# Gathered sums tied to an even beat in a planner that orders a graph layer's instructions

## The chip, the core and the metric

The kernel runs on one core of a Trainium2 chip, in one launch. Times are device microseconds (us) of that core. The core's engines are called as the profile calls them: PE (TensorE, with PEld for its weight loads), DVE (VectorE), ACT (ScalarE), POOL (GpSimd, which here issues the indirect loads) and SP (SyncE, which issues most plain loads and stores).

## The reference

One graph layer on 6250 nodes of 128 features, with 100000 edges sorted by their target `dst`; each edge has one of two types.

```python
Xs = X[src]
m_data = Xs @ W_data.T + b_data
m_ctrl = Xs @ W_control.T + b_control
msg = jnp.where((edge_types == 0)[:, None], m_data, m_ctrl)
agg = jax.ops.segment_sum(msg, dst, num_segments=X.shape[0])
out = relu(agg + (X @ W_self.T + b_self))
result = layernorm(x + out)        # no scale, no shift, eps 1e-5
```

## The kernel before

**A table first.** Both messages of all 49 blocks of 128 nodes are computed (`multiply`, L465) and split into three bfloat16 parts, so that a message is a row of 384 bfloat16 numbers. The rows stay on the chip as `m3` and are also stored to memory as `table`. This takes the first 80 us or so.

**Then 49 target blocks, in two ways.** An edge's message is added into its target's row by multiplying with a matrix of zeros and ones ("hot"); sums are accumulated in PSUM.

- Blocks 0 to 34, in seven groups of five, here called the p stream. Edges are first put into buckets by their source block (`ranks`, `fill_a`, `fill_b`, `fill_c`, on PE and DVE; few edges that don't fit are fetched by an indirect load, step `spilled`, L715). Then each block has 25 tiles: PE gathers 128 messages with a product out of `m3` (step `g`, tile `g_ps`, L775), ACT copies them from PSUM to `gs` (step `e`, L790; in the last five blocks DVE takes a part), and PE adds them up (step `s`, tile `agg`, L231).
- Blocks 35 to 48, here called the gathered stream: 14 blocks of 18 tiles, 252 in all. POOL fetches 128 rows of `table` by an indirect load (step `msg`, L877) into one of `MB = 5` buffers, DVE makes the hot matrix of six tiles at a time (step `gh`, L889), and PE adds (step `gm`, tile `agg_g`, L231). A tile's sum needs no copy by ACT, so these sums fill PE beside the p stream.

A step `g`, `s` or `gm` is four matmuls of 32 columns with 384 numbers each. After a block's last sum come `whole` and `sum` (DVE), and for each group `root` (DVE), `rooted` (ACT), `scale` (DVE), `apply` (ACT, one per block) and the store `out`. The gathered blocks are normalised in groups of 5, 5 and 4; of the p stream's last group, four blocks go first and block 34 goes alone.

**What sets the order.** Each engine executes its instructions in the order in which the program has them. That order comes from a small planner, the class `Order`, when the program is built. Every stream is a generator of steps; a step names its engines with costs in us, the steps that it needs, and a `lag` after its end. The planner keeps the time at which each engine is free (`self.free`), and always takes, among the steps of the earliest engine that could start within `CLOSE = 0.1` us of the first, the one with the smallest due time (function `due`). The costs, lags and due times exist in the planner alone: on the chip only the order and the real dependences are left.

For the gathered stream the planner before assumes that POOL needs `PACE = 1.68` us for a load, with the rows there 3.0 us after its start; a sum may be placed as soon as its rows are planned to be there, and its due time lies 5 us after its place in an even row. Each load needs the sum five back, whose buffer it takes:

```python
free = [("gm", *gathered[i - MB])] if i >= MB else [*stored, "idx"]
yield step(("msg", j, k), {"G": PACE}, *free, lag=3.0 - PACE)
```

Of the kernel before, what the change touches and what calls it, by code (L numbers as in the profile page):

```python
# [27 lines left out]
KT = 18  # L28
# [24 lines left out]
CH = 6  # L53
# [5 lines left out]
class Order:  # L59
# [10 lines left out]
    CLOSE = 0.1  # L70

    def __init__(self):
        self.free = dict.fromkeys("TVAGS", 0.0)
        self.end = {}

    def run(self, streams, due):
# [24 lines left out]
def step(name, costs, *needs, lag=0.0):  # L101
    return as_tuple(name), costs, [as_tuple(n) for n in needs], lag


def as_tuple(name):
    return name if isinstance(name, tuple) else (name,)
# [107 lines left out]
def sums_over_windows(ctx, tc, x, xt, edges, w, bias, table, packed, total,  # L214
                      add_parts, finish, load_rows, norm):
    nc = tc.nc
    V, A, G, T = nc.vector, nc.scalar, nc.gpsimd, nc.tensor
# [10 lines left out]
    def by_columns(out, lhsT, rhs, **flags):  # L228

        for c in range(0, P, 32):  # L230
            T.matmul(out[c : c + 32], lhsT[:, c : c + 32], rhs, **flags)  # L231
# [151 lines left out]

    LEAD, BUILT = 6.0, 76
    BLOCK = 13.1
    PACE = 1.68
    AHEAD, FIRST = 26.0, 20

    def due(kind, *i):
        if kind in ("p", "g") and i[0] in ("root", "rooted", "scale", "apply", "out"):  # L390
            n = i[1] + 1
            return BUILT + 10 + (BLOCK * sum(p[2] for p in PIECES[:n]) if kind == "p" else PACE * KT * GQ * n)
        if kind in ("counted", "turned", "first"):
            return 5.0
        if kind == "idx":
            return BUILT - 4
        if kind in ("stores", "built"):
            return BUILT - 6
        each = (BUILT - 8 - LEAD) / NB
        if kind == "xt":  # L400
            return LEAD - 6 + each * at_part[i[0]]
        if kind == "er":
            return 5.0
        if kind in ("total", "totalled"):
            return BUILT + BLOCK * (NPB - 1)
        if kind in ("set", "slots"):
            return 14.0
        if kind == "counts":
            return 9.0 if i[0] == GROUPS[0] else 30.0
        if kind == "set2":  # L410
            return 40.0
        kinds = ("y", "yh", "y1", "ym", "y2", "yl")
        if kind in kinds:
            return LEAD + each * i[0] + kinds.index(kind)
        if kind == "table":
            return LEAD + each * (at_part[i[0]] + PARTS[i[0]]) + 14
        if kind in ("win", "xs", "agg", "o", "whole", "sum"):
            b = i[0]
            begun = BUILT + (BLOCK * b if b < NPB else PACE * KT * (b - NPB))
            if kind == "win":  # L420
                return due("fields", blocks[b][0]) - 8 if b < NPB else BUILT - 20
            if b >= NPB:
                return begun + {"whole": PACE * KT + 2, "sum": PACE * KT + 5}.get(kind, 0)
            return begun + {"whole": BLOCK + 0.5, "sum": BLOCK + 3}.get(kind, 0.3 * BLOCK)
        if kind in ("rows", "sel", "d", "g", "e", "s"):
            of = {"rows": 1, "sel": 1, "d": 2}.get(kind, NS)
            lead = {"rows": -9, "sel": -3, "d": -1, "g": 0, "e": 1, "s": 2}[kind]
            return BUILT + BLOCK * (i[0] + (i[1] / of if len(i) > 1 else 0)) + lead
        if kind in ("gh", "gm", "msg"):
            k = i[1] * CH if kind == "gh" else i[1]  # L430
            return BUILT + PACE * (i[0] * KT + k) + {"msg": 0, "gh": 2, "gm": 5}[kind]
        n = GROUPS[i[0]]
        end = BUILT + BLOCK * STARTS[i[0]] - (AHEAD if i[0] else FIRST)
        span = BLOCK * n if i[0] else 34.0
        begun = end - span
        if kind == "fields":
            return begun - 8
        if kind == "hot":
            return begun + span * i[1] * KC / KT - 4
        if kind in ("tri", "rank", "rest"):  # L440
            return begun + span * i[1] / KT + {"tri": 0, "rank": 0.5, "rest": 1}[kind]
        if kind in ("two", "v"):
            c, k = (i[1], 0) if kind == "two" else divmod(i[1], KC)
            return begun + span * (c + 1) * KC / KT + (2 if kind == "two" else 3 + 0.3 * k)
        return end + ("vs", "vd", "to", "over", "pos", "codes", "posed", "list", "listed",
                      "spilled", "full").index({"packed": "vs"}.get(kind, kind))
# [68 lines left out]
    stored = [("table", g, t) for g in range(len(PARTS)) for t in range(2)]  # L515
# [337 lines left out]
    gathered = [(j, k) for j in range(NG) for k in range(KT)]  # L853
    idx = const.tile([P, NG, KT], I32, name="idx")
# [5 lines left out]
    def gathered_fields():  # L860
        yield step("idx", {"V": 1.8}, ("y", NB * 3 // 4), *[("win", b) for b in range(NPB, NB)])
        shape = [P, NG, KT]
        far = work.tile(shape, I32, name="far_g", bufs=1)
        V.tensor_scalar(far, win_g[:, :, :, 2], 0.0, float(NP), op0=ALU.not_equal, op1=ALU.mult)
        V.tensor_add(idx, far, win_g[:, :, :, 0])
        V.tensor_sub(rel_g, win_g[:, :, :, 1], base[:, NPB:, None].to_broadcast(shape))
        low = work.tile(shape, F32, name="low_g", bufs=1)
        V.tensor_single_scalar(low, rel_g, float(P), op=ALU.is_lt)
        V.scalar_tensor_tensor(low, rel_g, 0.0, low, op0=ALU.is_ge, op1=ALU.mult,
                               accum_out=counts[:, NPG : NPG + 1])  # L870

    def gather_rows():
        for i, (j, k) in enumerate(gathered):
            free = [("gm", *gathered[i - MB])] if i >= MB else [*stored, "idx"]
            yield step(("msg", j, k), {"G": PACE}, *free, lag=3.0 - PACE)
            msgs[j, k] = late.tile([P, D3], BF16, name="msg", bufs=MB)
            G.indirect_dma_start(  # L877
                out=msgs[j, k], out_offset=None, in_=table[:, :],
                in_offset=bass.IndirectOffsetOnAxis(ap=idx[:, j, k : k + 1], axis=0),
            )  # L880

    def gathered_hots():
        chunks = [(j, c) for j in range(NG) for c in range(KT // CH)]
        for i, (j, c) in enumerate(chunks):

            free = [("gm", chunks[i - XB][0], chunks[i - XB][1] * CH + CH - 1)] if i >= XB else []
            yield step(("gh", j, c), {"V": 0.55}, ("msg", j, c * CH), ("counts", CH), *free)
            g_hots[j, c] = hot = late.tile([P, P, CH], BF16, name="hot_g", bufs=XB)
            V.tensor_tensor(hot, counted[CH],  # L889
                            rel_g[:, j, None, c * CH : c * CH + CH].to_broadcast([P, P, CH]),  # L890
                            op=ALU.is_equal)

    def gathered_sums():
        for j, k in gathered:
            free = [("agg", NPB + j)] if k == 0 else [("o", NPB + j)] if k == KT - 1 else []
            yield step(("gm", j, k), {"T": 0.165}, ("msg", j, k), ("gh", j, k // CH), *free)
            if k == 0:
                aggs[NPB + j] = ps_a.tile([P, D3], F32, name="agg_g")
            by_columns(aggs[NPB + j], g_hots[j, k // CH][:, :, k % CH], msgs.pop((j, k)),
                       start=k == 0, stop=k == KT - 1, skip_group_check=True)  # L900

    def finish_gathered():
        for j in range(NG):
            b = NPB + j
            yield step(("whole", b), {"V": 0.5}, ("gm", j, KT - 1))
            whole = add_parts(aggs.pop(b), work)
            yield step(("sum", b), {"V": 0.7}, ("whole", b))
            if j % GQ == 0:
                kept.append((late.tile([P, GQ, D], F32, name="h_g"),
                             work.tile([P, Q, 2], F32, name="mv_g")))  # L910
            h, mv = kept[-1]
            finish(h[:, j % GQ, :], whole, xss.pop(b))
            stats(mv[:, j % GQ, :], h[:, j % GQ, :], work)
# [14 lines left out]
    def close_build():  # L928
# [9 lines left out]
        normalise([(lambda g=g: (hs_[g], mvs[g]), STARTS[g] + q0, q0, n) for g, q0, n in PIECES], "p"), add_up(), gather(), evict(), to_hots(), bucket_hots(),  # L938
        multiply(), take(0, "yh", "y"), leave(0, "y1", "yh"),
        take(1, "ym", "y1"), last_part(), constants(), store(), close_build(), add_counts(),  # L940
        finish_gathered(), gathered_sums(), gathered_hots(), gather_rows(), gathered_fields(),
        normalise([(lambda i=i: kept[i], NPB + i * GQ, 0, min(GQ, NG - i * GQ))
                   for i in range(-(-NG // GQ))], "g"),
        load_own("p", list(range(NPB)), XS),
# [128 lines left out]
```

## Time and profile before

| what | value |
|---|---|
| median of 13 runs | 544.62 us (542.65 to 546.29) |
| profiled execution: its own time | 543.5 us |
| profiled execution: span from first to last instruction | 541.8 us |
| mean granted TensorE clock over the span | 0.986 |
| busy share of the span: PE, PEld, DVE, ACT, POOL | 94%, 82%, 80%, 77%, 55% |
| indirect loads `msg` on POOL | 252, mean 1138 ns each on the engine |
| eviction `gs<-g_ps` on ACT | 807, mean 498 ns |

The busy share is an average over stages: the table until about 80 us, then both streams side by side until the last gathered sum at 517 us, then the end of the p stream. "Idle before" is the time for which an engine stood still ahead of an instruction, with what released it. A matmul's end is modelled, and consecutive matmuls overlap.

### The profile page before, as it was taken

The page shows a single profiled execution, that of the slowest core. Times are in us where ns is not written, and L with a number is a line of the kernel's source. Part 1 is how long each engine was busy: PE and PEld are TensorE (multiplying, and loading weights), DVE is VectorE, ACT ScalarE, POOL GpSimd, SP SyncE. Part 2 cuts the span into 40 slices and gives each one's busy share as a digit, 9 for nine tenths or more (in the row PEclk, how much of TensorE's full clock was granted, in tenths as well). Part 3 has the DMA queues.
Part 4 walks back from the last instruction along what each step waited for, and adds up shares of the span by engine and source line. Part 5 has one row for each costly group of instructions (what it writes and reads, how often), then busy time and mean ns, then how long its engine had stood idle before and what let it go on. Part 6 is the DMA issues. An engine that isn't in the chain of part 4 may idle for free.

```text
span 541.8 us, 26355 instructions
## 1 busy us (share of the span) xinstructions
PE 507.0 (94%) x11204; PEld 442.0 (82%) x11204; DVE 432.6 (80%) x967; ACT 416.0 (77%) x1003; POOL 295.9 (55%) x267
## 2 busy tenths in 40 slices
PE   5799977899989999999999999999999999999993
PEld 3546547799887998988989899989898999988882
DVE  5587879578987789978799878999789667668884
ACT  6654346577869788798888888977879879888894
POOL 1000002677687676777567676775757756676500
PEclk9999999899999999999999999999999999999998
DMA  3566875543555435554354543544445454555301
GB/s 98 142 177 200 259 235 187 153 130 79 184 153 166 136 78 178 158 162 141 98 194 137 165 141 80 183 139 158 142 132 162 130 159 135 182 168 156 116 14 38
DMA packets 60932, 79.19 MB, mean 146 GB/s; under 512 B 15760, under 2 KB 51371, under 8 KB 60807
## 3 DMA queue, kind: packets, MB, share of 16 engines
q1 hardware_dynamic: 47253, 49.14, 27.9%
q0 software_dynamic: 12400, 25.08, 17.7%
q10 hardware_dynamic: 1154, 3.21, 1.9%
q8 instruction: 89, 1.46, 1.1%
q14 instruction: 36, 0.29, 0.2%
HBM read 64.35 MB, written 13.05 MB: 143 GB/s over the span
## 4 chain that ended last, share of the span: by engine, by line
PE 76%; DMA 8%; DVE 7%; ACT 3%; issue 3%; POOL 1%; SPq 1%; ACTq 0%; DVEq 0%; POOLq 0%
PE agg L231 25%; PE g_ps L775 24%; PE acc L231 9%; PE agg_g L231 8%; PE small L621 7%; DMA msg<-table,idx 4%; DMA rows<-packed 3%; PE y L465 2%; DVE slot L584 2%; ACT gs L790 1%; DVE hot_st L567 1%; ACT h_p L189 1%; DVE two L605 1%; ACT h_g L189 1%; POOL msg L877 1%
## 5 line engine op out<-in xcount | busy, mean ns | idle before, releaser
L790 ACT CAST gs<-g_ps 128x384 bf16<-128x384 f32 x807 | 333.7, 498 | 74.7 <-PE g_ps L775 54.7
L877 POOL DMA_INDIRECT msg<-table,idx x252 | 286.8, 1138 | 118.1 <-PE g_ps L775 49.6
L775 PE MATMUL g_ps<-m,rows 128*32 128x384 bf16 x3430 | 322.3, 332 | 0.9 <-ACT gs L790 0.7
L231 PE MATMUL agg<-gs,hot_d 128*32 128x384 bf16 x3360 | 301.0, 330 | 3.3 <-ACT gs L790 3.3
L231 PEld LDWEIGHTS <-hot_d 128*32 128x32 bf16 x3500 | 194.6, 137 | 13.5 <-issue 7.2
L775 PEld LDWEIGHTS <-rows 128*32 128x32 bf16 x3430 | 188.5, 136 | 19.1 <-issue 13.3
L231 PE MATMUL agg_g<-msg,hot_g 128*32 128x384 bf16 x1008 | 109.4, 331 | 7.0 <-DMA msg<-table,idx 6.2
L584 DVE TENSOR_REDUCE slot<-acc 128x5 bf16<-128x490 f32 x126 | 83.5, 663 | 28.9 <-PE acc L231 17.3
L760 DVE TENSOR_TENSOR hot_d<-count,to 128x1664 bf16<-128x1664 bf16 x70 | 74.5, 1065 | 6.6 <-PE agg L231 6.6
L621 PE MATMUL small<-hot_st,two 128*32 128x98 bf16 x1260 | 70.2, 291 | 0.0
L231 PE MATMUL acc<-hot_st,tri 128*32 128x490 bf16 x504 | 62.2, 376 | 2.2 <-DVE hot_st L567 2.2
L231 PEld LDWEIGHTS <-hot_g 128*32 128x32 bf16 x1008 | 53.9, 123 | 11.6 <-issue 8.1
L231 PE MATMUL acc<-hot_st,rest 128*32 128x490 bf16 x476 | 56.7, 379 | 5.2 <-DVE slot L584 4.8
L621 PEld LDWEIGHTS <-two 128*32 128x32 bf16 x1260 | 58.8, 118 | 2.0 <-issue 0.3
L715 POOL DMA_INDIRECT mixed<-table,row_i x7 | 6.8, 969 | 92.9 <-PE g_ps L775 82.4
L476 ACT CAST m<-y 128x512 bf16<-128x512 f32 (+1 forms) x50 | 28.1, 577 | 30.8 <-PE y L483 23.0
L567 DVE TENSOR_TENSOR hot_st<-count,st_b 128x2940 bf16<-128x2940 bf16 x21 | 41.8, 1995 | 7.0 <-PE small L621 5.3
L746 DVE TENSOR_SCALAR rows<-rows,pid 128x3136 bf16<-128x3136 bf16 x35 | 37.2, 1062 | 7.6 <-DMA rows<-packed 6.1
L153 DVE TENSOR_REDUCE whole<-agg 128x128 f32<-128x384 f32 x35 | 19.4, 554 | 17.5 <-PE agg L231 12.4
L465 PE MATMUL y<-w_sb,xt 128*128 128x256 f32 x98 | 33.1, 424 | 0.0
L231 PEld LDWEIGHTS <-rest 128*32 128x32 bf16 x476 | 21.9, 99 | 13.6 <-issue 12.7
L231 PEld LDWEIGHTS <-tri 128*32 128x32 bf16 x504 | 22.4, 99 | 3.3 <-issue 3.1
(144 smaller groups left out, 436.7 us busy)
## 6 DMA issues: line engine op xcount, KB each, us to landing
rows<-packed SPq DMA_DIRECT2D x35, 784.0 KB
table<-m SPq DMA_DIRECT2D x10, 768.0 KB
msg<-table,idx POOLq DMA_INDIRECT x252
xt<-in_xt ACTq DMA_DIRECT2D x5, 512.0 KB
xt_p<-in_xt SPq DMA_DIRECT2D x35, 64.0 KB
xs_p<-in_x SPq DMA_DIRECT2D x35, 64.0 KB
out<-h_p SPq DMA_DIRECT2D x6, 320.0 KB
table<-m SPq DMA_DIRECT2D x2, 480.0 KB
```

What stands on the lines that cost most here:

```text
L153: nc.vector.tensor_reduce(whole, agg.rearrange("p (i c) -> p c i", i=3), axis=AX.X, op=ALU.add)
L231: T.matmul(out[c : c + 32], lhsT[:, c : c + 32], rhs, **flags)
L465: T.matmul(y[:, j, :], xts[g][:, b + j - at_part[g], :], w_sb[:, : 2 * D], start=j == 0, stop=False, skip_group_check=True)
L476: A.copy(part_of(b, n, i), ys[b][:, :n, :].rearrange("p b (t c) -> p t b c", t=2))
L567: V.tensor_tensor(hot, counted[n][:, None, 1 : NT + 1, :].to_broadcast([P, KC, NT, n]), fields[grp][2][:, c * KC : c * KC + KC, None, :].t ...
L584: V.tensor_reduce(slots[grp][:, k, :], by_q, axis=AX.X, op=ALU.max)
L621: T.matmul(vt[c0 : c0 + R, q // 2, :], two[:, k % KC, i, :, q], hot[:, k % KC, :, q], start=k == 0 and q < 2, stop=k == KT - 1, skip_group ...
L746: V.tensor_scalar(rows[b], rows[b], pid1, None, op0=ALU.is_equal)
L760: V.tensor_tensor(hot, counted[DC][:, :, :n], places[grp][:, q, None, c * DC : c * DC + n].to_broadcast([P, P, n]), op=ALU.is_equal)
L775: T.matmul(g_ps[t * R : (t + 1) * R, :D3], rows[b][:, :, s], m3[:, s, :], start=True, stop=True)
L790: (A.copy if e == "A" else V.tensor_copy)(gs[at], g_tiles.pop((b, g))[at, :D3])
L877: G.indirect_dma_start(out=msgs[j, k], out_offset=None, in_=table[:, :], in_offset=bass.IndirectOffsetOnAxis(ap=idx[:, j, k : k + 1], axis=0),
```

## The change

The planner gets a sixth, made-up engine "C". A new stream `beats` puts one step every `PACE` us on it, starting 4.0 us after the table's stores are planned to have landed. Each gathered sum needs its beat too, so that it is never planned earlier than that. `PACE` grows from 1.68 to 1.75; the planned cost of a load on POOL falls from 1.68 to 1.25 and its rows are planned to be there 4.25 us after its start; a sum's due time no longer lies 5 us behind its place. The beats issue nothing: the changed kernel has the same instructions on the chip in another order. The wait of each load for the sum five back was there before and is there after.

```diff
-        self.free = dict.fromkeys("TVAGS", 0.0)
+        self.free = dict.fromkeys("TVAGSC", 0.0)
...
-    PACE = 1.68
+    PACE = 1.75
...
+        if kind in ("beat", "beating"):
+            return 0.0
         if kind in ("gh", "gm", "msg"):
             k = i[1] * CH if kind == "gh" else i[1]
-            return BUILT + PACE * (i[0] * KT + k) + {"msg": 0, "gh": 2, "gm": 5}[kind]
+            return BUILT + PACE * (i[0] * KT + k) + {"msg": 0, "gh": 2, "gm": 0}[kind]
...
-            yield step(("msg", j, k), {"G": PACE}, *free, lag=3.0 - PACE)
+            yield step(("msg", j, k), {"G": 1.25}, *free, lag=3.0)
...
+    def beats():
+
+        yield step("beating", {"C": 4.0}, *stored, "idx")
+        for i, (j, k) in enumerate(gathered):
+            yield step(("beat", j, k), {"C": PACE}, "beating")
...
-            yield step(("gm", j, k), {"T": 0.165}, ("msg", j, k), ("gh", j, k // CH), *free)
+            yield step(("gm", j, k), {"T": 0.165}, ("msg", j, k), ("beat", j, k), ("gh", j, k // CH), *free)
...
-        finish_gathered(), gathered_sums(), gathered_hots(), gather_rows(), gathered_fields(),
+        finish_gathered(), gathered_sums(), gathered_hots(), gather_rows(), gathered_fields(), beats(),
```

## The prediction, made before the changed kernel ran

> **What bounds the kernel now.** I read the page's engine rows first, then busy time by stretches, then the list of waits, then PE's timeline around its longest wait, and last the chain of waits at the end. Busy time by stretches (columns: PE, PEld, DVE, ACT, POOL busy with counts, then PE's clock, DMA share, GB/s):
>
> ```profile
> 70.00:140.00 70.00, 62.19 (x1346) 52.94 (x1348) 56.24 (x120) 47.14 (x114) 36.14 (x30) 0.95 0.52 160
> 140.00:210.00 70.00, 67.66 (x1618) 60.79 (x1607) 58.59 (x131) 57.10 (x140) 50.60 (x44) 1.00 0.48 141
> 210.00:280.00 70.00, 68.34 (x1647) 62.58 (x1650) 59.98 (x139) 58.26 (x148) 49.27 (x43) 1.00 0.51 154
> 280.00:350.00 70.00, 69.20 (x1709) 65.00 (x1705) 60.60 (x132) 58.78 (x145) 49.28 (x44) 1.00 0.48 142
> 350.00:420.00 70.00, 68.31 (x1667) 62.72 (x1661) 61.74 (x135) 58.44 (x148) 47.91 (x44) 1.00 0.47 144
> 420.00:490.00 70.00, 69.24 (x1687) 64.22 (x1683) 49.24 (x113) 60.06 (x153) 45.64 (x44) 1.00 0.49 152
> ```
>
> From 140 us on PE stands still for 1 to 3.4% of the time; the next engines are DVE at 70 to 88% and ACT at 82 to 86%. The densest stretch issues 1709 matmuls in 70 us, 0.041 us each, so a step of four takes 0.164 us. Against that rate the stretches 140:210, 210:280, 350:420 and 420:490 lack 91, 62, 42 and 22 matmuls, 217 x 0.041 = 8.9 us (the mix of shapes differs a little, so this is rough). PE bounds the middle; what it waits there is carried to the end. The waits and the timeline of PE (start, duration, in brackets idle before and releaser) say for what:
>
> ```profile
> PE agg_g L231 <- DMA msg<-table,idx: 6.2, 5, 3.6
> PE agg L231 <- ACT gs L790: 3.3, 6, 1.0
> POOL msg L877 <- PE agg_g L231: 38.7, 59, 2.1
> ACT gs L790 <- PE g_ps L775: 54.7, 97, 5.3
> ```
>
> ```profile
> 91.48 0.35 PE L775 MATMUL g_ps<-m,rows 128*32 128x384 bf16 x4
> 95.43 0.38 PE L231 MATMUL agg_g<-msg,hot_g 128*32 128x384 bf16 x4 [3.60 <-DMA msg<-table,idx]
> 96.55 0.45 PE L231 MATMUL agg_g<-msg,hot_g 128*32 128x384 bf16 x4 [0.31 <-DMA msg<-table,idx]
> 105.19 0.38 PE L231 MATMUL agg_g<-msg,hot_g 128*32 128x384 bf16 x4 [0.56 <-DMA msg<-table,idx]
> ```
>
> The largest wait of PE in the two-stream part is for gathered rows: 6.2 us in 5 waits, one of 3.6 us before the very first sum. POOL in turn stands still for sums (38.7 us behind `agg_g`): the load waits for its buffer. And ACT waits for PE 54.7 us, far more than PE for ACT. At the end the chain of waits reads (start, length, what):
>
> ```profile
> 522.94 0.38 ACT h_g L189
> ...
> 523.85 0.49 ACT h_g L189
> ...
> 532.63 0.48 ACT mixed L790
> 533.16 0.41 PE agg L231 x4
> 533.59 0.57 DVE whole L153
> ...
> 535.24 0.21 ACT s L170
> ...
> 536.65 0.49 ACT h_p L189
> ```
>
> After the last gathered sum (517.3 us) evictions on ACT lead, and two of the gathered blocks' `apply` stand among them on the chain. The last eviction starts at 532.63 and ends at 533.10, `whole` of block 34 follows at 533.59, and its store is issued at 537.17, 4.07 us after that eviction.
>
> **The change, part by part.** No instruction is added or removed; costs, lag, beat and due time live in the planner. So the planned 1.25 us for a load costs nothing on POOL and neither does the wait for the sum five back, which the old program has as well. What changes is position, and that can be counted in the built order of PE, in matmuls.
>
> (a) The first gathered sum stands 26 matmuls later (878th instead of 852nd). 26 x 0.041 = 1.05 us of other work moves into the 3.6 us wait, if it is ready: the evictions that it needs run until about 92.5 us (ACT is busy 0.53 us of 92 to 94), while PE had stopped at 91.8. So PE arrives at about 92.8 instead of 91.8; the rows land at 95.4 as before, since the loads ahead of it keep their order. Gain 1.0 us, bounds 0 and 1.05.
>
> (b) The other four waits for rows, 6.2 - 3.6 = 2.6 us. From one gathered sum to the one five later, between which a load has to be issued and land, the old order has 102 matmuls at the least, and under 160 in 21 places of 247; the new order 148 at the least, under 160 in one. At 0.041 us that is 4.2 against 6.1 us. From the trace's semaphore times I read 2.4 to 6.8 us from issue to landing (median 3.6, nine in ten under 5.5), and 0.3 us from a sum's end to the issue. So nearly all gaps now exceed what a load takes. Gain 2.6 us, at least 1.0 (the waits after the first five tiles, 0.31 and 0.56, have 1 to 2.5 us more room), at most 2.6.
>
> (c) The clock. In 96 to 98 and 98 to 100 us the granted clock was 0.68 and 0.50, right after the 3.6 us wait; after the wait of 1.5 us at 159 us it stayed at 1.00. Half speed for 3.4 us costs up to 1.7 us. A wait of 2.6 us lies between those two, so the gain is 0 to 1.7; I take 0, as PE would still be idle from 92.8 to 95.4, most of the same stretch.
>
> The Trainium skill (TensorE: Matmul & The Clock Gate, HAM oscillation) names PE idle gaps over about 3.4 us as what throttles the clock. The row agrees; by the rule alone a wait of 2.6 us would be short enough and the sum below 1.7 us better.
>
> (d) All other waits of PE (3.3 us on evictions, some on `slot`) are dealt anew, since every step moves against every other. Even spacing should rather help: 13 times in the old order two gathered sums stand back to back, once in the new. Upper bound: the 8.9 us lacking in the middle less the 2.0 us of (b) that lie there, so about 7. Lower bound: nothing excludes a loss; the nearest rows are POOL's spilled loads, which hold up the loads behind them by up to 2.9 us, and one such wait hitting PE would cost that. I take 0, with 3 us either way.
>
> [...]
>
> (e) The end of the p stream. In the old order 348 matmuls follow the last gathered sum; they take from 517.3 to 533.5 us, 16.2 us or 0.0466 each, 2.0 us more than at full rate. In the new order 70 follow, so some seven gathered sums (0.164 us each) go into that slack, and the gathered blocks' `apply`, of which the chain has 0.87 us, leave it. Gain 0.9 us, bounds 0 and 2.0.
>
> (f) The last four gathered blocks are now finished at the very end. On DVE their `root` and `scale` stand ahead of `whole` of block 34, and on ACT their `rooted` stands behind the last eviction and their four `apply` ahead of block 34's `rooted`. With e the end of the last eviction, from the old chain's rows: `rooted` until e + 0.26, then 0.27 to the first of six DVE instructions and 1.13 through them, so `whole` at e + 1.7 instead of e + 0.49. Then 1.65 us to `rooted`, e + 3.35; ACT is busy with four `apply` (0.4 apart, the last 0.5 long) until e + 3.45. Then 1.93 us to the store as before, so e + 5.4 instead of e + 4.07. Cost 1.35 us, bounds 0.5 and 2.5. The gathered blocks' own store (245 KB) is issued at about e + 4 and lands some 2 us later (the 256 KB store issued at 531.88 stopped moving data at 533.9), before the last one.
>
> Sum: - 1.0 - 2.6 - 0 - 0 - 0.9 + 1.35 = - 3.15 us. On the profiled execution, 543.5 us (span 541.8 and 1.7 around it), that gives 540.4; this execution lies 1.1 us under the median of 544.62, so in medians 541.5 us. Adding all favourable bounds gives far less than 536, all unfavourable ones 544.62 + 0 - 1.0 + 3 + 2.5 = 549.1; both are unlikely in full.
>
> **Rivals.** *Eviction paces instead (slower).* If the p stream is held by the loop of four `g_ps` buffers and ACT, PE's saved waits come back as waits for `gs`, and (f) stays: 544.62 + 1.35 = 546.0. For it: ACT is at 84 to 86% and leads the end of the chain. Against: ACT waits 54.7 us for PE, PE 4.0 us for ACT. It decides once PE's waits on ACT grow by over 3.6 us, what (a) and (b) bring. Chance 0.22.
>
> *A larger gain.* The clock dip goes (1.7) and a third of the lacking 7 us is filled (2.3): 541.5 - 4.0 = 537.5. For it: 153 of the 217 lacking matmuls are lacking between 140 and 280 us, before the two streams have settled into the dense rate. Against: no wait of PE in the list but those for rows is that large. Chance 0.2.
>
> *It does nothing.* The order moves, but waits for rows reappear behind the spilled loads and take half of (b), and evictions take the rest of what (f) leaves: 544.6. Chance 0.14.
>
> **How the numbers follow.** My own case, 541.5 with 539 to 543.3, has 0.42; the larger gain 0.2, no change 0.14, slower 0.22, with 0.02 for surprises of over 3 us on the slow side. Two executions' medians can be told apart here at about 0.2%, 1.1 us. So faster 0.62, same 0.14, slower 0.24. The range reaches from 536.5 (a little beyond the larger gain) to 546.6 (just beyond the eviction case).
>
> **What would show it.** In the changed profile: PE's waits for `msg` down from 6.2 to about 2.6 us, all in the first; a first gathered sum still near 95.4 us; the last one some 3 to 4 us before PE's end, near 528; `whole` of block 34 1.7 us after the last eviction; the store 5.4 us after it. PE's waits for `gs` should stay near 3 to 4 us: if they reach 7, the eviction rival is right. A clock of 1.00 between 96 and 100 us would speak for the larger gain. If waits for `msg` stay at 6 us, (b) is wrong.

## The result and the profile after

The changed kernel's median is 538.1 us (10 runs, 536.57 to 538.64), against 544.55 us for the kernel before (46 runs, 541.58 to 546.4). The ratio is 0.9878 [0.9861, 0.9895], a gain of 6.45 us. The prediction had 541.5: the sign was right and the value lies inside the range, but the gain is more than twice the 3.15 us of the sum.

The profiled execution of the changed kernel took 538.18 us, its span 536.4 us, 5.4 us less than before. The remaining 1 us of the 6.45 is no change of mechanism: before's profiled execution lay 1.05 us under its own median, the changed one lies at its median. So what has to be explained in the traces is 5.4 us.

First, busy time by stretches of the changed kernel (columns as before: PE, PEld, DVE, ACT, POOL busy with counts, PE's clock, DMA share, GB/s):

```profile
70.00:140.00 70.00, 63.16 (x1380) 54.84 (x1383) 57.62 (x127) 48.92 (x120) 33.34 (x32) 0.95 0.51 163
140.00:210.00 70.00, 68.42 (x1661) 62.96 (x1655) 60.37 (x135) 58.67 (x144) 50.62 (x42) 1.00 0.50 149
210.00:280.00 70.00, 69.14 (x1659) 63.00 (x1655) 59.78 (x133) 58.74 (x147) 50.88 (x44) 1.00 0.50 147
350.00:420.00 70.00, 69.02 (x1713) 63.99 (x1709) 60.25 (x136) 60.32 (x150) 49.81 (x43) 1.00 0.50 149
490.00:520.00 30.00, 30.00 (x734) 28.32 (x730) 24.67 (x49) 23.77 (x56) 17.82 (x16) 1.00 0.38 111
```

PE executes more matmuls in the same time: 1380 instead of 1346 in the first of these stretches, 1661 instead of 1618 in the second, 1713 instead of 1667 in the fourth; 420:490 went the other way, from 1687 to 1653. In 490:520 it is 734, where before had 701:

```profile
490.00:520.00 30.00, 29.38 (x701) 25.63 (x697) 24.90 (x53) 25.35 (x61) 14.76 (x13) 1.00 0.38 117
```

The clock is the same in each of these stretches.

Second, the list of waits (total us, how many, the longest). The lines answer to those of before; the last one is POOL's wait ahead of the spilled loads, which the prediction did not show:

```profile
PE agg_g L231 <- DMA msg<-table,idx: 4.0, 1, 4.0
PE agg L231 <- ACT gs L792: 3.7, 6, 1.0
POOL msg L879 <- PE agg_g L231: 50.5, 75, 2.3
ACT gs L792 <- PE g_ps L777: 55.8, 87, 3.8
POOL mixed L717 <- issue: 1.2, 4, 0.3
```

PE waits for gathered rows once, before the first sum, and not again. Its waits for evictions moved from 3.3 to 3.7 us, so ACT did not become the bound. POOL waits longer for sums than before, 50.5 us against 38.7, at no cost to PE. Before, the spilled loads stood like this in the same view:

```profile
POOL mixed L715 <- DVE dq L712: 8.3, 4, 2.9
POOL mixed L715 <- DVE dq L711: 1.9, 1, 1.9
```

POOL takes its instructions in order. For 10.2 us it stood still at spilled loads whose list of rows DVE had not finished, and every gathered load behind them stood still too. After the change POOL is idle for 0.3 us ahead of each spilled load but the first group's, four of them in the line above.

Third, PE's timeline around its one wait (start, duration, in brackets idle before and releaser):

```profile
92.35 0.40 PE L231 MATMUL agg<-gs,hot_d 128*32 128x384 bf16 x4
96.74 0.38 PE L231 MATMUL agg_g<-msg,hot_g 128*32 128x384 bf16 x4 [3.99 <-DMA msg<-table,idx]
```

Last, the end of the chain of waits (start, length, what):

```profile
527.09 0.48 ACT mixed L792
...
528.05 0.57 DVE whole L153
...
529.70 0.21 ACT s L170
...
531.10 0.49 ACT h_p L189
```

The last eviction ends at 527.56, `whole` of block 34 starts 0.49 us later and its store is issued 4.07 us after that eviction. Before it was 0.49 and 4.07 us too. The four gathered blocks that are now finished here cost the end nothing.

**A finer reading than the list.** A matmul's end is modelled and consecutive matmuls overlap, so the list of waits counts only idle time beyond the modelled end. The trace also has starts. Below, a "start gap" is the time from the start of one matmul to the start of the next, less the 0.165 us of a whole step (0.21 us for the wider ones), where over 0.15 us is left, from 88 us on. How long a gap comes out depends on what is taken off, so the sums compare kernels better than they measure a loss. Before the change the start gaps ahead of gathered sums add up to 8.7 us, 3.76 ahead of the first one and 4.95 ahead of the others; after it 4.15 ahead of the first and nothing ahead of the others. All other start gaps of PE are 14.3 us before and 14.0 after.

### The profile page after: what moved, and what is told of

The parts are those of the page before. It is cut to its first block, busy times and chain, and to the rows that moved or that the text cites. A ratio compares the mean times of both kernels' runs of the same rounds, so it can differ in the third digit from the quotient of the medians.

```text
span 536.4 us, 26363 instructions
## 1 busy us (share of the span) xinstructions
PE 504.8 (94%) x11204; PEld 442.6 (83%) x11204; DVE 431.8 (80%) x968; ACT 416.8 (78%) x1002; POOL 300.8 (56%) x267
## 4 chain that ended last, share of the span: by engine, by line
PE 79%; DVE 9%; DMA 4%; ACT 3%; issue 2%; SPq 2%; ACTq 0%; DVEq 0%
PE agg L231 27%; PE g_ps L777 25%; PE acc L231 9%; PE agg_g L231 8%; PE small L623 7%; PE y L467 2%; DMA rows<-packed 2%; DVE hot_st L569 2%; ACT gs L792 2%; DVE slot L586 2%; ACT h_p L189 1%; DMA msg<-table,idx 1%; DVE two L607 1%; DMA packed<-vs 1%; SPq L809 1%
## 5 line engine op out<-in xcount | busy, mean ns | idle before, releaser
L879 POOL DMA_INDIRECT msg<-table,idx x252 | 290.4, 1153 | 125.4 <-PE g_ps L777 57.4
L777 PE MATMUL g_ps<-m,rows 128*32 128x384 bf16 x3430 | 318.6, 332 | 0.0
L231 PEld LDWEIGHTS <-hot_d 128*32 128x32 bf16 x3500 | 192.5, 137 | 13.6 <-issue 8.9
L231 PE MATMUL agg_g<-msg,hot_g 128*32 128x384 bf16 x1008 | 112.4, 329 | 4.0 <-DMA msg<-table,idx 4.0
L623 PE MATMUL small<-hot_st,two 128*32 128x98 bf16 x1260 | 68.6, 291 | 0.5 <-DVE two L607 0.4
L231 PE MATMUL acc<-hot_st,tri 128*32 128x490 bf16 x504 | 60.6, 374 | 2.3 <-DVE hot_st L569 2.3
L623 PEld LDWEIGHTS <-two 128*32 128x32 bf16 x1260 | 57.0, 118 | 3.4 <-DVE two L607 1.8
L717 POOL DMA_INDIRECT mixed<-table,row_i x7 | 8.1, 1158 | 84.9 <-PE g_ps L777 83.1
L792 DVE CAST gs<-g_ps 128x384 bf16<-128x384 f32 x34 | 18.5, 554 | 8.8 <-PE g_ps L777 5.3
```

The costliest lines, as they stand in the source:

```text
L623: T.matmul(vt[c0 : c0 + R, q // 2, :], two[:, k % KC, i, :, q], hot[:, k % KC, :, q], start=k == 0 and q < 2, stop=k == KT - 1, skip_group ...
L777: T.matmul(g_ps[t * R : (t + 1) * R, :D3], rows[b][:, :, s], m3[:, s, :], start=True, stop=True)
L792: (A.copy if e == "A" else V.tensor_copy)(gs[at], g_tiles.pop((b, g))[at, :D3])
L879: G.indirect_dma_start(out=msgs[j, k], out_offset=None, in_=table[:, :], in_offset=bass.IndirectOffsetOnAxis(ap=idx[:, j, k : k + 1], axis=0),
```

## Experiments

The theory after this reading: the gain is PE's waits for gathered rows, and they vanish for two reasons, because there is more distance between a sum and the one five later (what the prediction had), and because POOL's queue is no longer held up by spilled loads. The rivals: one part of the change does it alone (the pace, or the planned costs without the beat); more buffers would do the same; any new order would have done it; the first wait and the clock decide.

### Which part of the change

**The old pace with all the rest of the change.**

```diff
-    PACE = 1.75
+    PACE = 1.68
```

> The changed kernel with PACE back at 1.68: sums of gathered tiles still on an even beat, but as early as before (412 matmuls follow the last one, 348 in the old kernel, 70 in the changed one). Shortest distance to the sum five later 154 matmuls (old 102, changed 148). Theory, evenness removes PE's waits for gathered rows: most of the gain stays, 4 to 6 us faster than before, waits for rows down to the first one. Rival, the slower pace fills the end of the p stream: at most 1 us faster. Rival, any new order is a draw: anything between -3 and +3 us.

Measured: 539.02 us, 0.9893 [0.9867, 0.9919]. The new pace isn't needed; the interval overlaps that of the whole change, and POOL is idle for 0.3 us ahead of each late spilled load here too.

**The new pace alone, on the kernel before.**

```diff
-    PACE = 1.68
+    PACE = 1.75
```

> The old kernel with PACE 1.75 alone, without beats, old costs and due times: the sums run as late as in the changed kernel (the last one stands at the very end) but unevenly (distance to the sum five later at least 136 matmuls, under 160 in 13 places; old 102 and 21, changed 148 and 1). Theory, evenness: some of the waits for rows stay; 1 to 2 us faster from them, less what the last gathered block now costs at the very end, so -2 to +2 us. Rival, pace and a filled end: 4 to 6 us faster.

Measured: 546.36 us, 1.0038 [1.0018, 1.0058]. By itself the pace costs a little. PE ended at 531.9 us, earlier than before's 533.5, but the last gathered sum stood at the very end of the order, and from PE's end to the end of the span it took 13.4 us instead of 8.3. POOL's wait at the spilled loads was 11.7 us.

**Planned costs, lag and due time, without the beat.** On the changed kernel:

```diff
-    PACE = 1.75
+    PACE = 1.68
...
-            yield step(("gm", j, k), {"T": 0.165}, ("msg", j, k), ("beat", j, k), ("gh", j, k // CH), *free)
+            yield step(("gm", j, k), {"T": 0.165}, ("msg", j, k), ("gh", j, k // CH), *free)
```

> The changed kernel without the beats and with PACE 1.68: planned cost of a load 1.25 and due time not set back, so sums are placed as soon as rows are planned to be there. Distances to the sum five later grow less even (under 150 matmuls in 37 places, 8 in the old kernel). Theory, evenness: waits for rows stay at 6 us or grow; 0 to 5 us slower than before. Rival, the planner's truer costs bring the gain: 4 to 6 us faster.

Measured: 546.07 us, 1.0019 [0.9992, 1.0046]: no gain. PE's waits for rows rose to 11.3 us in 9 waits:

```profile
PE agg_g L231 <- DMA msg<-table,idx: 11.3, 9, 4.3
POOL mixed L717 <- issue: 0.9, 3, 0.3
```

In the built order 53 of the 247 distances to the sum five later are under 160 matmuls, against 21 before and 1 after. Without the beat the planner bunches the sums. POOL, on the other hand, no longer stands at the spilled loads: ahead of each of the six late ones it is idle for 0.3 us. So it is the planned costs, not the beat, that move these out of the way, and that alone does not help.

**The beat, with the old planned cost of a load.** On the changed kernel:

```diff
-            yield step(("msg", j, k), {"G": 1.25}, *free, lag=3.0)
+            yield step(("msg", j, k), {"G": PACE}, *free, lag=3.0 - PACE)
```

> The changed kernel, with beats and PACE 1.75, but POOL planned as before: a load costs PACE and its rows are there 3.0 us after its start. In the built order the sums are less even again (seven back to back, at least 114 matmuls to the sum five later, three places under 160) and 18 matmuls follow the last one. Theory, evenness and the place of the spilled loads in POOL's queue both count: POOL waits for the spilled loads' indices return (8 to 12 us, none in the changed kernel), some waits of PE for rows return; 1 to 4 us slower than the changed kernel. Rival, the beat alone does it: within 1 us of the changed kernel.

Measured: 548.23 us, 1.0071 [1.0046, 1.0096]. The spacing is nearly as even as after (3 distances under 160), but the kernel is slower than before. Part of it is the tail, 11.4 us from PE's end to the end of the span instead of 8.3. More shows in the list of waits:

```profile
PE agg_g L231 <- DMA msg<-table,idx: 10.1, 9, 4.4
POOL mixed L717 <- DVE dq L714: 13.7, 5, 3.4
```

POOL stands 13.7 us behind spilled loads. They execute at 274.72, 341.30, 408.75 and 474.47 us after waits of 2.4 to 3.4 us, and 5 to 6 us after each of them, at 280.8, 346.3, 413.7 and 480.3, PE has a start gap ahead of a gathered sum whose rows come last. So even spacing alone does not do it; these four gaps are the second cause caught in the act.

### Spilled loads and buffers

**Eight buffers, all orders as before.**

```diff
-    MB, XB = 5, 2
+    MB, XB = 8, 2
```

> The old kernel with MB = 8 buffers for gathered rows in place of 5. Every engine's order of instructions is that of the old kernel, only loads may go earlier. Theory, the gain is the waits for rows: PE's waits for rows fall to the first one, and the time falls by what they really cost, 2.6 us by the list of waits, up to 5 us by the gaps between matmul starts. Rival, the gain is the new order itself (evictions, tail): at most 1 us faster.

Measured: 542.44 us, 0.9965 [0.9945, 0.9985], 1.9 us less than before. The built order is that of before on every engine; a load now waits for the sum eight back. If the distance of five were all, the waits for rows would have gone. They stayed at 6.5 us in 6, and POOL, which now can run ahead, ran into the spilled loads:

```profile
POOL mixed L715 <- DVE dq L712: 37.7, 6, 7.5
```

The lead that POOL gains is used up there, and PE's gaps at 213 and 480 us, ahead of gathered sums behind a spilled load, are 0.7 and 0.55 us; before had 0.4 us (in two) and 0.4 us there. All start gaps ahead of gathered sums fell from 8.7 to 7.8 us, about half of the gain; where the other half comes from the trace does not show.

**Eight buffers in the changed kernel** (the same edit).

> The changed kernel with eight buffers for gathered rows in place of five, planned with eight too (two places with under 160 matmuls to the sum five later, 70 matmuls become 86 after the last gathered sum). Theory, in the new order no wait for rows but the first is left, so more room brings nothing: within 1.5 us of the changed kernel, 4.5 to 8 us faster than before. Rival, loads that go earlier always help: 1.9 us faster than the changed kernel, as eight buffers were in the old order.

Measured: 538.35 us, 0.9886 [0.9868, 0.9905]. Once the waits are gone, more buffers bring nothing that can be measured.

**Spilled loads four gathered loads later, all else as before.** Only POOL's order differs from before:

```diff
+    HOLD, held = 4, []
...
-            G.indirect_dma_start(
-                out=mixed[grp % 2][:R], out_offset=None, in_=table[:, :],
-                in_offset=bass.IndirectOffsetOnAxis(ap=row_i[:, 0:1], axis=0),
-            )
+            if grp:
+                held.append([HOLD, mixed[grp % 2][:R], row_i])
+            else:
+                spill(mixed[grp % 2][:R], row_i)
...
+            for one in list(held):
+                one[0] -= 1
+                if not one[0]:
+                    held.remove(one)
+                    spill(*one[1:])
```

> The old kernel, with each spilled load (but the first group's) put four gathered loads later in POOL's queue. Every other engine's order is the old one. Theory, the spilled load at the head of POOL's queue, waiting for its indices from DVE (8.3 and 1.9 us in the old trace), holds up the loads behind it and so makes rows late: POOL's wait for dq falls under 1 us, PE's gaps before gathered sums fall from 8.7 to about 5 us, 2 to 4 us faster than before. Rival, rows are late because sums stand too close together: within 1 us of before.

Measured: 541.79 us, 0.9947 [0.9926, 0.9969], 2.8 us less than before. POOL's wait for `dq` is gone; PE's waits for rows fell from 6.2 to 5.1 us in the list, its start gaps ahead of gathered sums from 8.7 to 6.7, and PE ended 1.5 us earlier, at 532.0. The profiled execution, 542.36 us, gained less than the median; its clock was at half for 6.8 us behind the first wait, before's for 3.4. This is the second cause by itself.

**Spilled loads seven gathered loads later, with eight buffers.** `HOLD` is 7 and `MB` is 8, all else as before.

> As the last one, with eight buffers for gathered rows and the spilled loads seven loads later; all other orders are the old ones. Here rows can hardly be late after the first tiles, whatever the spacing of the sums. Theory, late rows are what the change took away: 3 to 5 us faster than before, PE's gaps before gathered sums near 4.5 us, all at the first tiles. Rival, the new order gains by its even mix of both streams: at most 2 us faster, as eight buffers alone.

Measured: 540.47 us, 0.9923 [0.9894, 0.9952], 4.1 us less than before.

```profile
PE agg_g L231 <- DMA msg<-table,idx: 4.9, 3, 3.5
```

The waits for rows that are left are those of the first three late tiles (3.67 at 94.2, 0.48 at 95.5, 1.08 at 104.3 us); after 105 us no rows were waited for. So with before's order of PE untouched, distance and a free POOL queue bring about two thirds of the gain. (That both together bring more than the later loads alone, 541.79 us, shows in the traces; the two intervals overlap.) About 1 us of what is left to the changed kernel is those first tiles, 5.2 us against 4.2; the other us or so is inside the intervals.

**The beat with the old load cost, and spilled loads four later.** The kernel of 548.23 us, with `HOLD = 4`:

> The kernel with beats and the old planned cost of a load (548.2 us, PE's gaps before gathered sums 12.9 us), with each spilled load four gathered loads later in POOL's queue. Theory, held-up loads cost it: 3 to 6 us faster than without this, so 542 to 545 us; the rest of its loss is its end, where the gathered blocks' normalisation stands behind the last sums. Rival, its uneven sums cost it: within 1.5 us of 548.2.

Measured: 544.57 us, 1.0011 [0.9989, 1.0033], 3.7 us less than without the delay by the medians, 3.3 us by the two ratios. PE's waits for rows fell from 10.1 to 4.7 us, none of the four gaps named above is there, and PE ended at 528.2 us, as early as in the changed kernel (528.0). (The comparison with 538.0 in the kernel without the delay would say too much: of the two profiled executions that one, 551.46 us, was among its slowest, this one, 541.55, its fastest.) What it still loses in its trace is the tail: the last gathered sum stands at the very end of its order (18 matmuls follow it in the same plan), and from PE's end to the end of the span it takes 11.4 us. The 3 us from there to its median no trace shows.

### The first wait, the clock, the pace

**First beat later.** On the changed kernel the beats start 10.0 instead of 4.0 us after the stores, with `PACE` 1.72 in the first of these kernels and 1.68 in the second; the third and fourth start at 8.0 with 1.68 and at 6.0 with 1.75. The edit of the second:

```diff
-    PACE = 1.75
+    PACE = 1.68
...
-        yield step("beating", {"C": 4.0}, *stored, "idx")
+        yield step("beating", {"C": 10.0}, *stored, "idx")
```

> The changed kernel with the first beat 10 us instead of 4 us after the stores and PACE 1.72: the first gathered sum stands 96 matmuls later (974th), distances to the sum five later are as even (one place under 160), 170 matmuls follow the last one. Theory, the first wait of 4 us is PE time lost: it falls to under 1 us and the half-speed stretch behind it with its 1.7 us may go; 2 to 5 us faster than the changed kernel. Rival, before the first sum ACT's evictions pace the p stream anyway, so PE waits for ACT in place of rows: within 1.5 us of the changed kernel.

Measured: 539.75 us, 0.991 [0.9892, 0.9927].

> Beats with PACE 1.68, the first beat 10 us after the stores instead of 4: the first gathered sum is the 974th matmul instead of the 878th, 388 matmuls follow the last one (412 with the first beat at 4 us, 539.0 us). Theory, the first wait of 4 us and the half-speed stretch behind it are lost PE time: first wait under 1 us, clock 1.00 between 92 and 104 us, 1.5 to 4 us faster than with the first beat at 4 us, so 535 to 537.5 us. Rival, ACT's evictions pace the p stream there: PE's gaps before g_ps and agg grow by what the first wait loses, 538 to 540 us.

Measured: 537.93 us, 0.9875 [0.9845, 0.9906].

> As the last one, with the first beat at 8 us: the first gathered sum is the 934th matmul. Theory, lost PE time: the first wait about halved, no half-speed stretch if it is under 2 us; between 536 and 538.5 us. Rival, evictions pace: 538 to 540 us.

Measured: 539.83 us, 0.9901 [0.9869, 0.9932].

> The changed kernel with the first beat at 6 us instead of 4: first gathered sum the 914th matmul, no place under 160 matmuls to the sum five later, 54 matmuls after the last one. Theory, lost PE time: the first wait about 1.5 us shorter, 0.5 to 2 us faster than the changed kernel's 538.1. Rival, evictions pace, or the later end gives it back: 538 to 540 us.

Measured: 537.59 us, 0.9867 [0.9825, 0.9909].

None of the four can be told apart from the changed kernel, though the first wait is down to 1.7 us or less in all of them and the clock stays at 1.00. Two windows around it, first of the kernel with the old pace (first beat at 4.0), then of the one with 10.0 and the same pace:

```profile
96.00:100.00 4.00, 4.00 (x64) 2.62 (x57) 0.77 (x2) 1.40 (x4) 2.90 (x4) 0.63 0.40 108
```

```profile
96.00:100.00 4.00, 4.00 (x108) 3.88 (x107) 3.89 (x6) 2.33 (x7) 2.73 (x4) 1.00 0.55 133
```

From 92 to 100 us PE started 64 matmuls in the one and 163 in the other, so some 99 x 0.041 = 4.1 us of work was done earlier. At 94 us block 0 was done, 5.2 us before the other's 99.2; block 32 was done at 510.1 and 510.8. The lead was lost on the way: PE's start gaps ahead of `g_ps` are 9.9 us instead of 6.5 and those ahead of `acc` grew to 3.3, and all start gaps together are 19 us in both. So in these two traces the first wait, 4 us long, was worth 0.6 us at PE's end (529.1 and 528.5 us) and in the medians about 1 us, with intervals that leave room for 2 us more or less. That the p stream is paced by its four `g_ps` buffers and ACT in the early part would explain it, but no run isolates that. The fourth kernel's trace looks better: it has 15.8 us of start gaps in all, and PE ended at 522.8 us, 5.2 us before the changed kernel's. But this execution, 534.79 us, was one of its fastest (its runs go from 533.97 to 541.15), and its median gains nothing that can be told from none. So what the first wait costs stays open.

**The pace 1.72, first beat as in the change.**

```diff
-    PACE = 1.75
+    PACE = 1.72
```

> The changed kernel with PACE 1.72: 244 matmuls follow the last gathered sum (70 at 1.75, 412 at 1.68), seven places under 160 matmuls to the sum five later. Theory, with beats and true load costs the pace matters little: 537.5 to 539.5 us, as at 1.68 (539.0) and 1.75 (538.1). Rival, each order is a draw of its own: over 541 us or under 536.5 us.

Measured: 542.73 us (539.03 to 546.78), 0.9971 [0.9941, 1.0]. This misses what the theory expected. Its profiled execution, at 546.3 us near the top of its spread, has PE's waits for rows at 5.6 us in 4 and 24.8 us of start gaps in all, against 18.2 in the changed kernel and 19 to 21 in those with a later first beat and the paces 1.68 and 1.72. The pace itself is not bad, since 1.72 with a later first beat gave 539.75. All other kernels here that have both the beat and the new load cost lie between 537.6 and 539.8; this one falls out by 3 to 5 us, and the cause is open. It sets a limit to the theory: an order that does all that the change asks for can still lose most of the gain.

### The end

**The square root behind the evictions.** In the code `root` issues two instructions: an addition on DVE and the square root on ACT. The planner's step `rooted` comes after it and issues nothing. On the changed kernel, the square root is moved into that step:

```diff
-            v, s0 = root(mv, n, work)
+            v = root(mv, n, work, at_once=False)
             yield step((last, "rooted", grp), {"A": 0.3}, (last, "root", grp))
+            s0 = work.tile([P, Q], F32, name="s0")
+            A.activation(s0[:, :n], v[:, :n], AF.Sqrt)
```

> The changed kernel with the square root emitted with the step rooted instead of with root, which is where the prediction took it to be; on ACT it then stands one to three evictions later in every normalised group, and behind the last eviction in the gathered blocks' last group; no other engine's work is added or removed. Theory, this is why part (f) of the prediction cost nothing: whole of block 34 starts about 1.7 us after the last eviction's end instead of 0.5, the store is issued about 5.4 us after it instead of 4.07, and the time is 1.0 to 1.6 us longer than the changed kernel's. Rival, the end was covered by something else: no change.

Measured: 539.23 us (534.65 to 540.82), 0.9885 [0.9849, 0.9922], so in medians it can't be told from the changed kernel. The trace tells them apart. ACT's timeline of the changed kernel:

```profile
526.42 0.27 ACT L170 ACTIVATE s<-v 128x4 f32<-128x4 f32 x1
526.53 0.53 ACT L792 CAST gs<-g_ps 128x384 bf16<-128x384 f32 x1
527.09 0.47 ACT L792 CAST mixed<-g_ps 64x384 bf16<-64x384 f32 x1
527.95 1.65 ACT L189 ACTIVATE h_g<-h_g,shift,rstd 128x128 f32<-128x128 f32 x4 [0.39 <-DVE shift L184]
529.70 0.20 ACT L170 ACTIVATE s<-v 128x1 f32<-128x1 f32 x1
```

and of the kernel with the square root moved:

```profile
527.33 0.47 ACT L794 CAST mixed<-g_ps 64x384 bf16<-64x384 f32 x1
527.83 0.21 ACT L848 ACTIVATE s<-v 128x4 f32<-128x4 f32 x1
529.29 1.65 ACT L191 ACTIVATE h_g<-h_g,shift,rstd 128x128 f32<-128x128 f32 x4 [1.25 <-DVE shift L186]
530.84 0.19 ACT L848 ACTIVATE s<-v 128x1 f32<-128x1 f32 x1
```

In the changed kernel the gathered blocks' square root (`128x4`) stands ahead of the last two evictions, so its six DVE instructions run beside them, and the four `apply` are done at 529.60, just when block 34's square root is due. With the root behind the last eviction (end e = 527.81) `whole` of block 34 comes at e + 1.36 instead of e + 0.49, and the store at e + 4.94 instead of e + 4.07: 0.87 us. That is the collision which the prediction charged, in a kernel where it does happen.

## Why the prediction was right or wrong

**What bounds the kernel** was right. PE bounds the middle, what it waits there is carried to the end (4.95 us of start gaps ahead of the later gathered sums gone, PE's last matmul 5.5 us earlier, at 528.0 instead of 533.5), and ACT did not take over: PE's waits for `gs` went from 3.3 to 3.7 us, not to 7.

**(a) The first wait: - 1.0 forecast, + 0.4 measured.** PE arrived where it was expected: its last work before the wait ended at 92.75, predicted about 92.8. The step that failed is "the rows land at 95.4 as before, since the loads ahead of it keep their order". The first load was issued at 92.3 instead of 91.7 and took 4.4 instead of 3.7 us to land, at 96.7; in 94 to 96 us the DMAs moved 345 GB/s against 95 before. On POOL the loads did keep their order, but SP's order changed too. SP's next load of `rows`, 784 KB, came after the first sum before, and now comes together with the first gathered load (SP's timeline, before and after):

```profile
98.40 0.33 SPq L739 DMA_DIRECT2D rows<-packed  x1
```

```profile
92.29 0.33 SPq L741 DMA_DIRECT2D rows<-packed  x1
```

All kernels divide by this. In the eight whose first gathered sum stands where the change puts it, `rows` is issued within 1 us of the first gathered load, and that load's rows are used 4.4 to 5.3 us after its issue. In the five that keep before's place, `rows` comes 6 to 7 us later, and it is 2.8 to 3.7 us. No run moves that load by itself. In the kernels with a later first beat, a first wait that is gone altogether brought no time that could be told from none.

**(b) The other waits for rows: - 2.6 forecast, - 4.95 measured. This is the term that was mis-sized, and the step of it that failed is "6.2 - 3.6 = 2.6 us" with its bound "at most 2.6".** The list of waits was read as all that PE loses ahead of gathered sums. By start gaps before's 4.95 us consist of 1.07 in the first five tiles (96.6 and 105.2 us) and 1.5 at 159.5 us, which are in the list and make the 2.6; of 1.0 at 210.0, 214.3, 283.7 and 477.6 us, 1.5 to 8.3 us behind a spilled load, each too short for the list; and of 1.4 ahead of gathered sums that an engine released, 1.0 of it for the hot matrices at 410.0 and 500.0 us. All of it went. So rows account for 3.6 us of the 4.95, and the rest are waits that the term did not count. The 1.5 us at 159.5 us fits the spilled loads too: after the one at 140.8 us POOL issued the next 12 gathered loads with no more than 0.3 us of idle time ahead of each, so it had hardly caught up.

The mechanism was half of it. "Nearly all gaps now exceed what a load takes" is right, and without the beat the waits double (11.3 us). But the forecast took from it that distance is enough, and had the spilled loads only as a possible loss, in (d) and in a rival. The beat with the old load cost has the distance and is slower than before; the spilled loads four later have none of it and gain 2.8 us. Both parts of the change are needed: the truer planned cost of a load lets the planner set the spilled loads where DVE is done with them (without the beat POOL is idle for 0.3 us ahead of each, with the beat and the old cost for 13.7 us in all), and the beat keeps the distance.

**(c) The clock: 0 forecast, 0 measured.** The first wait stayed, and with it half the clock for 3.4 us, from 97.0 us on. The forecast's bound for it, 1.7 us, isn't refuted: the four kernels in which the clock stayed at 1.00 have medians from 0.5 us below the changed kernel's to 1.7 us above it, with intervals of 1 to 2.3 us either way.

**(d) Everything dealt anew: 0 forecast, - 0.3 measured** (14.3 to 14.0 us of start gaps). In the other kernels the same sum runs from 12.2 to 19.8 us, 2.1 below and 5.5 above before's, so the range of 3 us either way was too narrow on the side of a loss.

**(e) The end of the p stream: - 0.9 forecast.** In 490:520 us 33 more matmuls were executed than before, 33 x 0.041 = 1.35 us; part of that is rows no longer waited for, so the rest of PE's 5.5 us, 5.5 + 0.4 - 4.95 - 0.3 = 0.65, is the better measure. The size was about right. It wasn't tried by itself.

**(f) The gathered blocks at the end: + 1.35 forecast, 0 measured.** The step that failed is "`rooted` until e + 0.26", the square root behind the last eviction. It was read from the planner's step; the instruction is issued one step earlier, in `root`. With the root where the forecast had put it, the cost is 0.87 us, within its bounds of 0.5 and 2.5. The last gathered sum ended at 524.0 us, 4.0 before PE's end, as "some 3 to 4 us before PE's end" had it; "near 528" was off since PE's end came earlier.

With the measured sizes the sum is + 0.4 - 4.95 - 0.3 - 0.65 + 0 = - 5.5 us, and the span lost 5.4. The last term is what was left of PE's end, so that the sum closes on PE is by construction; what was not is that the tail behind PE added nothing.

**The rivals.** *Eviction paces instead* is refuted at its own point of decision: waits for `gs` grew by 0.4 us, not 3.6. It may hold near 100 us, where a saved first wait came back in the trace with the first beat at 10.0; no run isolates it. *A larger gain* had the time (537.5) for the wrong reason: the clock dip stayed, and the work that went in between 140 and 280 us was the waits for rows themselves. *It does nothing* named the right mechanism, waits behind spilled loads, with the wrong sign for this order: they went to 0.3 us each. It is what happens with the old load cost.

## What to carry to other kernels

Read an engine's loss to a cause from the starts of its instructions and not from the list of waits alone, where ends are modelled and short gaps don't count. In a queue that executes in order, look at each instruction that waits at its head for something unrelated: moving it a few places later was worth 2.8 of the 6.45 us here. More buffers without that were worth 1.9 us, and made the queue stand longer, 37.7 us instead of 10.2. When an edit moves a step of a hand-written planner, find the line that issues the instruction, as a step's name can stand one place behind what it is named for.

## What the runs showed that was not expected

- An indirect load with its list not ready held POOL for up to 7.5 us, with eight buffers 37.7 us in all, although the loads behind it were ready to go: the 13 loads after the longest of these waits followed with 0.3 us of idle time each.
- A first wait of PE of 3.5 to 4.4 us was followed by half the clock, mostly for 3.4 us, in three kernels for 6.8 us; waits of up to 1.7 us left it at 1.00. The Trainium skill (TensorE: Matmul & The Clock Gate, HAM oscillation) puts the limit at idle gaps of about 3.4 us, and the runs agree as far as they go, since none has a first wait between 1.7 and 3.5 us. But keeping the clock at 1.00 there brought no time at the end that could be told from none.
- Two orders of the same instructions that differ only in a planner's pace, 1.72 and 1.75, are 4.6 us apart in their medians, and the slower one spreads over 7.8 us from run to run where the other spreads over 2.1.
